# One tile in 128 of a graph kernel's gathered rows fetched by SyncE, a row at a time, and spilled blocks fetched two blocks ahead

## The chip, the cores and the metric

The kernel runs on one NeuronCore of a Trainium2 chip. Its time is the device time of one execution in microseconds (us), given as the median of three runs. A profile is one further execution, recorded by the hardware profiler, with a time of its own.

The engines are named as in the profile: PE (TensorE), DVE (VectorE), ACT (ScalarE), POOL (GpSimd) and SP (SyncE). SP computes nothing; it issues copies between DRAM and on-chip memory, each of which waits in SP's queue until its semaphores allow it. POOL issues the indirect copies (gathers), whose row addresses stand in a column of 128 numbers on chip.

## What is computed

A graph with 12500 nodes of 96 features and 412500 edges, sorted by destination. Each edge takes the source node's row, the destination node's row and four edge numbers through a linear layer with ReLU; the result is normalised over all edges and summed by destination:

```
node_feat = mlp(x, W_node, ...)                       # (12500, 96)
edge_feat = mlp(edge_attr, W_edge, ...)               # (412500, 96)
message   = concat([x[src], x[dst], edge_feat])       # (412500, 288)
message   = mlp(message, W_msg, ...)                  # (412500, 96)
agg       = segment_sum(message, dst, 12500)
x         = layernorm(x + agg + node_feat)
# mlp(h): h = relu(h @ W + b); gamma * (h - mean) * rsqrt(var + eps) + beta, over the rows
```

## The kernel before

**Tables.** The product of the message layer is split by its three inputs. `p_tab` holds x @ W_msg[source part] for all nodes, `q_tab` the same for the destination part, both in DRAM. An edge then needs one row of `p_tab` (384 bytes) by its source number. The source rows are scattered, so they are gathered; destination rows are neighbours, since the edges are sorted.

**Tiles, groups, blocks.** 128 edges are a tile, four tiles a group (`GT` = 4, 512 edges), four groups a block (`BG` = 4). There are 3223 tiles, 806 groups (`NG`) and 202 blocks. `gather(g, pg)` (L168) issues one gather of 128 rows on POOL for each tile of group g (L172).

**Stages.** While the tables and the statistics of nodes and edges are computed (up to about 630 us), POOL gathers the first 26 blocks and SP writes them back to DRAM (`spill`, 768 KB a block, L183). `SPILL` = 104 is the number of groups so treated. Then POOL fills a ring of `RING` = 21 group buffers (`ring`, tile `pg`, L341 and L364), and the message stage begins.

**The message stage** goes over all 202 blocks in the order `order`: the 176 blocks that are gathered late, with the 26 spilled ones strewn among them, one after about every seven. The order of the instructions on all engines is the one written in the loop (L523 to L547). For each step k, that is group g of the block at place s:

- at the first group of a block, `load(s + 2)` on SP: edge numbers (L408, L410, one set for two late blocks), then a register load of the block's first node (L413) and with it a copy of rows of `q_tab` into one of three slots of `rhs` (L418), which waits until PE has used the slot. Then `fetch(s + 1)`: if that block is a spilled one, its 768 KB come back from DRAM into one of two buffers `pb` (L425).
- `linear(k + 1)` on PE (L464), one group ahead, and `message(k)`: DVE adds the gathered rows (L475, tile `hs`), ACT applies the ReLU once a block (L482). `edges(s + 1)` (L450) and `prepare(s + 1)` (L457) make the next block's inputs of `linear`.
- `sums(k - 4)` on PE (L497) sums by destination, and `add` on DVE (L510, L511) adds a block's sums to the whole, two blocks later.
- if g is a late group, the gathers of group `ahead` = g + 21 (nearly; the last lines of the loop) into the ring slot that group g has just left.

Every copy that SP issues takes one of eight semaphores in turn and waits for the copy that had it before; POOL's gathers have eight others.

After the loop follow the statistics of the messages and the output in 13 pieces (L720 to L755). `general()` is a second way for other inputs, which these inputs don't take.

Of the kernel before, what the change touches and what calls it, by code (L numbers as in the profile page):

```python
# [11 lines left out]
F32 = mybir.dt.float32  # L12
I32 = mybir.dt.int32
# [3 lines left out]
ET = mybir.EngineType  # L17
# [3 lines left out]
N, C, E, ED = 12500, 96, 412500, 4  # L21
EPS = 1e-5
P = 128
# [3 lines left out]
GT, GE, BG = 4, 512, 4  # L27
NT = -(-E // P)
NG = -(-NT // GT)
NBL = -(-NG // BG)  # L30
NTP, NGP = NBL * BG * GT, NBL * BG
EP = NGP * GE
# [19 lines left out]
SPILL = 26 * BG  # L52
RING = 21
# [2 lines left out]
HB, RB = 2, 3  # L56
CL, CE = 2, 2
BUSY = 4
J = 8


# [12 lines left out]
def gnn(ctx, tc, t):  # L74
    nc = tc.nc
    const = ctx.enter_context(tc.tile_pool(name="const", bufs=1))
    dram = ctx.enter_context(tc.tile_pool(name="dram", bufs=1, space=DRAM))
    p_tab = dram.tile([NN, C], F32, name="p_tab")
# [11 lines left out]
    ring = rpool.enter_context(tc.tile_pool(name="ring", bufs=RING))  # L90
# [16 lines left out]
    wide = const.tile([P, P], F32, name="wide")  # L107
# [57 lines left out]
                (nc.scalar if (c // CH + k) % 2 else nc.sync).dma_start(outs[k][:, c:c + CH, :], r[:, :, k, :])  # L165
            yield

    def gather(g, pg):  # L168
        tab, idx = (t["x"], src_raw) if g < RAW * BG else (p_tab, src)
        for i in range(min(GT, NT - g * GT)):  # L170
            k = g * GT + i
            nc.gpsimd.indirect_dma_start(  # L172
                out=pg[:, i, :], out_offset=None, in_=tab[:, :],
                in_offset=bass.IndirectOffsetOnAxis(ap=idx[:, k:k + 1], axis=0))
        return pg
# [110 lines left out]
    def edge_norm():  # L286

        with tc.tile_pool(name="es", bufs=2) as work, tc.tile_pool(name="es1", bufs=1) as one, \
                tc.tile_pool(name="es_ps", bufs=4, space=PSUM) as ps:
            stats = one.tile([P, NS, NBL, 6], F32, name="estats")  # L290
            for b in range(NBL):
                if b % J == 0:
                    yield
                    ea = work.tile([P, J, GE], F32, name="ea")
                    n = min(J, NBL - b)
                    for i in range(NS):
                        nc.sync.dma_start(ea[Q * i:Q * i + 2 * EK, :n, :],
                                          t["ea"][EK * i:EK * (i + 2), b:b + n, :])
                for i in range(NS):
                    k = NS * b + i  # L300
                    if k % 2 == 0:
                        pr = ps.tile([P, 2, GE], F32, name="pr")
                    nc.tensor.matmul(pr[:, k % 2, :], wide[Q * i:Q * i + 2 * EK, :],  # L303
                                     ea[Q * i:Q * i + 2 * EK, b % J, :], start=True, stop=True)
                    if k % 2:
# [32 lines left out]
            nc.vector.tensor_scalar(w_e, w_msg[:, 2, :], a_e, None, op0=OP.mult)  # L338

    def fast(ring):  # L340
        def ahead_of(g):  # L341
            return gather(g, ring.tile([P, GT, C], F32, name="pg"))

        with tc.manual_schedule(engines={ET.SP, ET.Pool}):
            nc.sync.dma_start(q_tab[:WM, :], zero[:WM])
# [18 lines left out]
            got = {g: ahead_of(g) for g in range(SPILL, SPILL + RING)}  # L364
# [3 lines left out]
        order = []  # L368
# [7 lines left out]
        with tc.tile_pool(name="fix", bufs=1) as fix, tc.tile_pool(name="msg", bufs=2) as work, \  # L376
# [22 lines left out]
            def load(s):  # L399

                b = order[s]
                first = SPILL // BG
                c, o = ((b - first) // CL * CL + first, CL) if b >= first else (b // CE * CE, CE)
                if c not in eas:
                    o = min(o, NBL - c)
                    eas[c] = work.tile([P, o, GE], F32, name="ea" if b >= first else "eae")
                    for i in range(BG):
                        nc.sync.dma_start(eas[c][Q * i:Q * i + EK, :, :], t["ea"][EK * i:EK * (i + 1), c:c + o, :])  # L408
                    for i in range(2):
                        nc.sync.dma_start(eas[c][EK + i:P:Q, :, :], rel_d[i][:, c * BG * GE:(c + o) * BG * GE]  # L410
                                          .rearrange("o (b g e) -> (o g) b e", g=BG, e=GE))
                ea = eas[c][:, b - c, :]
                _, val = nc.values_load_multi_w_load_instructions(  # L413
                    base[:, b:b + 1], engines=[ET.SP], min_val=0, max_val=N - 1,
                    skip_runtime_bounds_check_because="they are nodes' numbers")
                rows = q_tab[bass.ds(val[0], WN), :]
                rows = bass.AP(rows.tensor, rows.offset, [[C, WN], [WS * C, BG], [1, C]], None, rows.runtime_checks)
                nc.sync.dma_start(rhs[C:C + WN, s % RB, :, :], rows)  # L418
                block[s] = ea

            def fetch(s):
                b = order[s]
                if b * BG < SPILL:
                    back = work.tile([P, BG, GT, C], F32, name="pb")
                    nc.sync.dma_start(back, spill[b].rearrange("p g (a c) -> p g a c", a=GT))  # L425
                    for i in range(BG):
                        got[b * BG + i] = back[:, i, :, :]
# [18 lines left out]
            def edges(s):  # L446

                prs[s] = ps.tile([P, BG, GE], F32, name="pr", bufs=1)
                for i in range(min(BG, NG - order[s] * BG)):
                    nc.tensor.matmul(prs[s][:C + WN, i, :], we[Q * i:Q * i + EK + 2, :],  # L450
                                     block[s][Q * i:Q * i + EK + 2, :], start=True, stop=True)

            def prepare(s):

                n = min(BG, NG - order[s] * BG)
                pr, x = prs[s], left[s % 2]
                nc.scalar.activation(x[:C + WN, :n, :], pr[:C + WN, :n, :], AF.Relu)  # L457

            def linear(k):
                s, g = steps[k]  # L460
                n = min(GT, NT - g * GT)
                zs[k] = zb[k % 2][:, :GT * C].rearrange("p (t c) -> p t c", c=C)
                for i in range(n):
                    nc.tensor.matmul(zs[k][:, i, :], left[s % 2][:KR, g % BG, i * P:(i + 1) * P],  # L464
                                     rhs[:KR, s % RB, g % BG, :], start=True, stop=True)

            def message(k):
                s, g = steps[k]
                n = min(GT, NT - g * GT)
                i = g % BG  # L470
                h, z, pg = hb[s % HB], zs.pop(k), got.pop(g)
                if i == 0:
                    four[0] = work.tile([P, BG, GT, C], F32, name="hs")
                hs = four[0]
                nc.vector.tensor_add(hs[:, i, :n, :], z[:, :n, :], pg[:, :n, :])  # L475
                if i == min(2, NG - 1 - (g - i)):
                    b = g - i
                    nc.vector.tensor_tensor(  # L478
                        h[:, :, :, C + 1:C + 1 + WN], rel[:, b:b + BG, :].unsqueeze(3).to_broadcast([P, BG, GT, WN]),
                        nodes_of.unsqueeze(2).to_broadcast([P, BG, GT, WN]), op=OP.is_equal)  # L480
                if i == BG - 1 and n == GT:
                    nc.scalar.activation(h[:, :, :, :C], hs, AF.Relu)  # L482
                elif i == BG - 1 or g == NG - 1:
                    for o in range(i + 1):
                        m = GT if o < i else n
                        nc.scalar.activation(h[:, o, :m, :C], hs[:, o, :m, :], AF.Relu)
# [13 lines left out]
            def add(s):  # L500
# [9 lines left out]
                    nc.vector.tensor_tensor(to, pa[:, i:n:2, C + 1:C + 1 + WN], to, op=OP.add)  # L510
                nc.vector.tensor_add(gram[:, :n, :], pa[:, :n, :C + 1], gram[:, :n, :])  # L511

            n, ahead = len(steps), SPILL + RING
            with tc.manual_schedule(engines={ET.SP, ET.Pool, ET.PE, ET.DVE, ET.Activation}):
                load(0)
                fetch(0)
                load(1)
                edges(0)  # L520
                prepare(0)
                linear(0)
                for k in range(n + SKEW):  # L523
                    s, g = steps[min(k, n - 1)]
                    if k < n and g % BG == 0:
                        if s + 2 < len(order):
                            load(s + 2)
                        if s + 1 < len(order):
                            fetch(s + 1)
                    if k + 1 < n:  # L530
                        linear(k + 1)
                    if k < n:
                        message(k)
                    if 0 <= k - BG < n:
                        sums(k - BG)
                    if k < n and s + 1 < len(order):
                        if g % BG == 0:
                            edges(s + 1)
                        if g % BG == 2:
                            prepare(s + 1)  # L540
                        if g % BG == 3 and order[s + 1] < RAW:
                            convert(s + 1)
                    if k >= SKEW and (k - SKEW) % BG == 0:
                        add((k - SKEW) // BG)
                    if k < n and g >= SPILL and ahead < NG:
                        got[ahead] = ahead_of(ahead)
                        ahead += 1  # L547

            d = fix.tile([C, BG, C], F32, name="d")
            s = fix.tile([C, 3], F32, name="s")  # L550
# [167 lines left out]
    with tc.tile_pool(name="fin", bufs=2) as work, tc.tile_pool(name="fin_ps", bufs=2, space=PSUM) as ps:  # L718

        busy = ps.tile([P, GE], F32, name="busy", bufs=1)  # L720
        for i in range(BUSY):
            nc.tensor.matmul(busy, ident, rel[:, i * P:(i + 1) * P, :].rearrange("p g t -> p (g t)"), start=True, stop=True)  # L722
# [67 lines left out]
```

## Time and profile before

| what | us |
|---|---|
| median of three runs | 4114.34 |
| lowest and highest | 4112.78, 4116.98 |
| the profiled execution | 4124.01 |
| its span, first to last instruction | 4122.3 |
| busy in the span: POOL, PE, DVE, ACT | 3072.2, 2875.0, 1245.9, 1035.6 |
| gathers of `pg`, 2807 | 2654.7 busy, 0.946 each |
| start of the first and the last gather of `pg` | 555.7, 4066.0 |
| first and last add of gathered rows (L475) | 633.5, 4068.8 |
| mean granted clock of PE | 0.728 of full speed |

The span is the time from the first to the last recorded instruction; the execution's own time lies 1.7 us above it. The share of busy time is a mean over stages: which wait ends last in a stage is read from the groups, whose lines give the busy time, the mean of one, the idle time just before them, and what ended most of it. An L with a number is a line of the kernel; a q behind an engine means its queue, where copies are issued. DMA share is the mean busy share of the 16 DMA engines.

### The profile page before, as it was taken

To read this page: it belongs to the slowest core of one execution; us is meant where nothing else is said; L and a number is where in the kernel's file an instruction comes from. 1 tells how busy PE (TensorE), PEld (TensorE's weight loads), DVE (VectorE), ACT (ScalarE), POOL (GpSimd) and SP (SyncE) were. 2 spreads that over 40 slices of the span, in tenths; PEclk is the share of its full clock that TensorE was granted. 3 is DMA by queue.
4 is the path that set the end of the run, shared out by engine and by line. 5 is a ranking of instruction groups with operands and counts; after the bars stand their busy time and mean duration, and the time that the engine had idled before them with its cause. 6 is when DMAs were issued, how large, how long until landed. Compare 5 with 4: busy or idle time off the path is not lost. (4 is left out here: it accounts for less than half of the span.)

```text
span 4122.3 us, 46288 instructions
## 1 busy us (share of the span) xinstructions
PE 2875.0 (70%) x16517; PEld 2372.3 (58%) x16517; DVE 1245.9 (30%) x2410; ACT 1035.6 (25%) x804; POOL 3072.2 (75%) x3244
## 2 busy tenths in 40 slices
PE   4699968776667766666576667766777667666666
PEld 4455537666556655655565556666666556555555
DVE  2599983222122222222122212221222122221223
ACT  1387753221112211111122111121211122211112
POOL 6777777777777777777777777777777777777775
PEclk7655558877677778778777777776777677878777
DMA  8555532222222222222222222222222222222224
GB/s 241 170 115 110 106 78 67 48 54 54 53 53 47 54 52 47 53 55 54 52 47 54 52 54 46 54 55 52 46 54 54 53 46 54 54 52 47 54 53 114
DMA packets 190373, 274.29 MB, mean 67 GB/s; under 512 B 121571, under 2 KB 121956, under 8 KB 189126
## 3 DMA queue, kind: packets, MB, share of 16 engines
q0 software_dynamic: 103136, 158.62, 18.4%
q1 hardware_dynamic: 71684, 99.14, 8.8%
q10 hardware_dynamic: 15312, 13.47, 1.2%
q8 instruction: 133, 2.18, 0.2%
q14 instruction: 108, 0.88, 0.1%
HBM read 227.55 MB, written 43.43 MB: 66 GB/s over the span
## 5 line engine op out<-in xcount | busy, mean ns | idle before, releaser
L172 POOL DMA_INDIRECT pg<-p_tab,src x2807 | 2654.7, 946 | 856.9 <-issue 766.0
L464 PE MATMUL z<-rhs,left 128*128 128x96 f32 x6446 | 1172.6, 341 | 1050.8 <-issue 613.3
L464 PEld LDWEIGHTS z<-rhs,left 128*128 128x128 f32 x6446 | 1063.0, 250 | 1312.7 <-issue 718.6
L475 DVE TENSOR_TENSOR hs<-z,pg 128x384 f32<-128x384 f32 x702 | 391.4, 557 | 2510.5 <-DMA pg<-p_tab,src 2199.7
L497 PE MATMUL pa<-h 128*97 128x128 f32 x6446 | 1112.4, 330 | 12.5 <-ACT h L482 9.0
L497 PEld LDWEIGHTS pa<-h 128*97 128x97 f32 x6446 | 989.7, 212 | 18.5 <-ACT h L482 15.2
L482 ACT ACTIVATE h<-hs 128x1536 f32<-128x1536 f32 x201 | 298.1, 1483 | 2018.3 <-DVE hs L475 2018.3
L457 ACT ACTIVATE left<-pr 127x2048 f32<-127x2048 f32 x202 | 378.4, 1873 | 716.8 <-PE pr L450 716.8
L172 POOL DMA_INDIRECT stage<-p_tab,src x368 | 352.8, 959 | 127.9 <-issue 107.7
L303 PE MATMUL pr<-ea,wide 10*128 10x512 f32 x1212 | 372.0, 1062 | 18.8 <-DMA ea<-in_ea 18.8
L309 DVE BATCH_NORM_STATS2 estats<-r 128x6 f32<-128x512 f32 x606 | 361.3, 676 | 25.5 <-ACT r L307 25.5
L307 ACT ACTIVATE r<-pr 128x1024 f32<-128x1024 f32 x303 | 293.1, 1024 | 141.8 <-PE pr L303 117.9
L303 PEld LDWEIGHTS pr<-ea,wide 10*128 10x128 f32 x1212 | 198.2, 319 | 191.3 <-ACT r L307 85.3
L450 PE MATMUL pr<-ea,we 7*127 7x512 f32 x1404 | 229.6, 725 | 12.8 <-DMA ea<-rel_d 12.8
L478 DVE TENSOR_TENSOR h<-rel,z 128x496 f32<-128x496 f32 x202 | 133.4, 660 | 0.0
L511 DVE TENSOR_TENSOR gram<-pa,gram 97x388 f32<-97x388 f32 x202 | 111.3, 551 | 0.0
L510 DVE TENSOR_TENSOR agg<-pa,agg 97x62 f32 x404 | 90.0, 223 | 36.8 <-PE pa L497 20.8
L475 DVE TENSOR_TENSOR hs<-z,pb 128x384 f32<-128x384 f32 x104 | 57.7, 555 | 114.7 <-PE z L464 114.7
L450 PEld LDWEIGHTS pr<-ea,we 7*127 7x127 f32 x1404 | 61.4, 205 | 43.2 <-issue 23.4
L172 POOL DMA_INDIRECT stage<-in_x,src_raw x48 | 45.6, 949 | 27.3 <-issue 10.7
L275 PE MATMUL py<-center,xp 96*128 96x96 f32 x196 | 42.8, 423 | 31.5 <-ACT xp L270 18.5
L275 PEld LDWEIGHTS py<-center,xp 96*128 96x128 f32 x196 | 42.0, 332 | 32.3 <-ACT xp L270 18.9
(113 smaller groups left out, 501.4 us busy)
## 6 DMA issues: line engine op xcount, KB each, us to landing
pg<-p_tab,src POOLq DMA_INDIRECT x2807
spill<-stage SPq DMA_DIRECT2D x26, 768.0 KB
pb<-spill SPq DMA_DIRECT2D x26, 768.0 KB
ea<-in_ea SPq DMA_DIRECT2D x75, 160.0 KB
rhs<-q_tab SPq DMA_DIRECT2D x202, 46.5 KB
ea<-in_ea SPq DMA_DIRECT2D x352, 20.0 KB
stage<-p_tab,src POOLq DMA_INDIRECT x368
y_d<-y0s SPq DMA_DIRECT2D x12, 384.0 KB
```

The lines of the kernel that those rows point to most:

```text
L172: nc.gpsimd.indirect_dma_start(out=pg[:, i, :], out_offset=None, in_=tab[:, :], in_offset=bass.IndirectOffsetOnAxis(ap=idx[:, k:k + 1], ax ...
L303: nc.tensor.matmul(pr[:, k % 2, :], wide[Q * i:Q * i + 2 * EK, :], ea[Q * i:Q * i + 2 * EK, b % J, :], start=True, stop=True)
L307: nc.scalar.activation(r, pr, AF.Relu)
L309: nc.vector.bn_stats(stats[:, (k - o) % NS, (k - o) // NS, :], r[:, 1 - o, :])
L450: nc.tensor.matmul(prs[s][:C + WN, i, :], we[Q * i:Q * i + EK + 2, :], block[s][Q * i:Q * i + EK + 2, :], start=True, stop=True)
L457: nc.scalar.activation(x[:C + WN, :n, :], pr[:C + WN, :n, :], AF.Relu)
L464: nc.tensor.matmul(zs[k][:, i, :], left[s % 2][:KR, g % BG, i * P:(i + 1) * P], rhs[:KR, s % RB, g % BG, :], start=True, stop=True)
L475: nc.vector.tensor_add(hs[:, i, :n, :], z[:, :n, :], pg[:, :n, :])
L478: nc.vector.tensor_tensor(h[:, :, :, C + 1:C + 1 + WN], rel[:, b:b + BG, :].unsqueeze(3).to_broadcast([P, BG, GT, WN]), nodes_of.unsqueeze ...
L482: nc.scalar.activation(h[:, :, :, :C], hs, AF.Relu)
L497: nc.tensor.matmul(pas[s][:, g % BG, :C + 1 + WN], h[:r, i, :C + 1], h[:r, i, :C + 1 + WN], start=i == 0, stop=i == n - 1)
L511: nc.vector.tensor_add(gram[:, :n, :], pa[:, :n, :C + 1], gram[:, :n, :])
```

## The change

The fourth tile of one group in 32 (`SG`), beginning with group 125, is not gathered by POOL. SP fetches its 128 rows with 128 copies of one row. Their numbers come as one row of the new input `rows` (the source numbers, a tile to a row) into `lin`, 128 numbers in the first row of the tile `wide`, which is not used otherwise any more at that point. A register load on SP takes 16 numbers (`SR`) into registers, and 16 copies use them as addresses. This is done at every second group (`SS`), so eight times in 16 of the 32 groups, at the end of the step, on SP's queue. After the last 16 the next tile's numbers are asked for. A period that would reach beyond the last group is left to POOL altogether.

Besides, `fetch` is called for the block two places on in the order, where it was one.

```diff
--- before.py
+++ after.py
@@ -56,6 +56,8 @@
 HB, RB = 2, 3
 CL, CE = 2, 2
 BUSY = 4
+SR, SS = 16, 2
+SG = 8 * BG
 J = 8
 
 
@@ -165,9 +167,9 @@
                 (nc.scalar if (c // CH + k) % 2 else nc.sync).dma_start(outs[k][:, c:c + CH, :], r[:, :, k, :])
             yield
 
-    def gather(g, pg):
+    def gather(g, pg, without=0):
         tab, idx = (t["x"], src_raw) if g < RAW * BG else (p_tab, src)
-        for i in range(min(GT, NT - g * GT)):
+        for i in range(min(GT, NT - g * GT) - without):
             k = g * GT + i
             nc.gpsimd.indirect_dma_start(
                 out=pg[:, i, :], out_offset=None, in_=tab[:, :],
@@ -338,8 +340,8 @@
             nc.vector.tensor_scalar(w_e, w_msg[:, 2, :], a_e, None, op0=OP.mult)
 
     def fast(ring):
-        def ahead_of(g):
-            return gather(g, ring.tile([P, GT, C], F32, name="pg"))
+        def ahead_of(g, without=0):
+            return gather(g, ring.tile([P, GT, C], F32, name="pg"), without)
 
         with tc.manual_schedule(engines={ET.SP, ET.Pool}):
             nc.sync.dma_start(q_tab[:WM, :], zero[:WM])
@@ -510,13 +512,28 @@
                     nc.vector.tensor_tensor(to, pa[:, i:n:2, C + 1:C + 1 + WN], to, op=OP.add)
                 nc.vector.tensor_add(gram[:, :n, :], pa[:, :n, :C + 1], gram[:, :n, :])
 
+            lin = wide[0:1, :].bitcast(I32)
+
+            def row_numbers(g):
+
+                nc.sync.dma_start(lin, t["rows"][g * GT + GT - 1:g * GT + GT, :])
+
+            def rows_of(pg, lo, hi):
+                _, val = nc.values_load_multi_w_load_instructions(
+                    lin[:, lo:hi], engines=[ET.SP], min_val=0, max_val=N - 1,
+                    skip_runtime_bounds_check_because="they are nodes' numbers")
+                for p in range(lo, hi):
+                    nc.sync.dma_start(pg[p:p + 1, GT - 1, :], p_tab[bass.ds(val[p - lo], 1), :])
+
 
 
             n, ahead = len(steps), SPILL + RING
+            row_numbers(ahead)
             with tc.manual_schedule(engines={ET.SP, ET.Pool, ET.PE, ET.DVE, ET.Activation}):
                 load(0)
                 fetch(0)
                 load(1)
+                fetch(1)
                 edges(0)
                 prepare(0)
                 linear(0)
@@ -525,8 +542,7 @@
                     if k < n and g % BG == 0:
                         if s + 2 < len(order):
                             load(s + 2)
-                        if s + 1 < len(order):
-                            fetch(s + 1)
+                            fetch(s + 2)
                     if k + 1 < n:
                         linear(k + 1)
                     if k < n:
@@ -543,7 +559,15 @@
                     if k >= SKEW and (k - SKEW) % BG == 0:
                         add((k - SKEW) // BG)
                     if k < n and g >= SPILL and ahead < NG:
-                        got[ahead] = ahead_of(ahead)
+                        m = (ahead - SPILL - RING) % SG
+                        if m == 0:
+                            by_row = ahead if ahead + SG <= NG else None
+                        got[ahead] = ahead_of(ahead, int(ahead == by_row))
+                        if by_row is not None and m % SS == 0 and m // SS * SR < P:
+                            lo = m // SS * SR
+                            rows_of(got[by_row], lo, min(lo + SR, P))
+                            if m // SS * SR == P - SR and by_row + 2 * SG <= NG:
+                                row_numbers(by_row + SG)
                         ahead += 1
 
             d = fix.tile([C, BG, C], F32, name="d")
@@ -764,6 +788,7 @@
     s, d = np.asarray(inputs["src"]), np.asarray(inputs["dst"])
     d = np.pad(d, (0, EP - E), mode="edge")
     give("src", np.pad(s, (0, EP - E)).reshape(NTP, P).T)
+    give("rows", np.pad(s, (0, EP - E)).reshape(NTP, P))
     give("dst", d.reshape(NTP, P).T)
     base = d[::GE * BG]
     give("base", base.reshape(1, NBL))
```

With the new lines L168, L172, L408 to L425, L464 and L475 of the kernel before are L170, L174, L410 to L427, L466 and L477 of the changed one; the table of numbers is loaded at L519, the registers at L522, the rows at L526.

## The prediction

> **What bounds the kernel now.** I read the busy line of the page first, then the costliest groups, then POOL's own waits, then the gathers stage by stage, and last SP's queue, which takes over the work. The first two (columns of a group: busy us, mean ns of one, idle before, its releaser):
>
> ```profile
> PE 2875.0 (70%) x16517; PEld 2372.3 (58%) x16517; DVE 1245.9 (30%) x2410; ACT 1035.6 (25%) x804; POOL 3072.2 (75%) x3244
> L172 POOL DMA_INDIRECT pg<-p_tab,src x2807 | 2654.7, 946 | 856.9 <-issue 766.0
> L475 DVE TENSOR_TENSOR hs<-z,pg 128x384 f32<-128x384 f32 x702 | 391.4, 557 | 2510.5 <-DMA pg<-p_tab,src 2199.7
> ```
>
> POOL is not busy all the time, 75%, and PE nearly as much. But DVE's add, which starts every group, sat 2199.7 us waiting for gathered rows, and the gathers waited for nothing: 2654.7 + 856.9 = 3511.6 us for 2807 of them is 1.251 us from one to the next, and the idle 0.305 us of each is "issue". POOL's waits and its timeline say the same (waits: us in total, times, longest; timeline: start, duration):
>
> ```profile
> POOL pg L172 <- issue: 766.0, 2512, 0.3
> POOL pg L172 <- DMA pg<-p_tab,src: 82.1, 266, 1.3
> POOL pg L172 <- DVE hs L475: 5.2, 17, 0.3
> ...
> 2002.32 0.94 POOL L172 DMA_INDIRECT pg<-p_tab,src  x1 [0.30 <-issue]
> 2003.57 0.95 POOL L172 DMA_INDIRECT pg<-p_tab,src  x1 [0.30 <-issue]
> 2003.77 0.56 DVE L475 TENSOR_TENSOR hs<-z,pg 128x384 f32<-128x384 f32 x1 [4.59 <-DMA pg<-p_tab,src]
> 2004.82 0.95 POOL L172 DMA_INDIRECT pg<-p_tab,src  x1 [0.30 <-DMA pg<-p_tab,src]
> ```
>
> The waits put down to a DMA or to DVE are the same 0.30 us: 82.1/266 and 5.2/17 are 0.31 us each, so nothing holds POOL. By stage (us, busy us of the gathers and their count, clock, DMA share, GB/s):
>
> ```profile
> 200.00:300.00 100.00, 74.01 (x80) 0.50 0.60 116
> ...
> 600.00:1000.00 400.00, 302.43 (x321) 0.76 0.24 56
> 1000.00:1500.00 500.00, 378.02 (x401) 0.76 0.23 51
> 3500.00:4000.00 500.00, 378.03 (x401) 0.79 0.23 52
> ```
>
> The pace is the same from the first to the last stage, 1.25 us, also where DMA is 60% busy. So the end is one chain: gathers of p_tab from 76 to 4067 us with hardly a gap (3175 x 1.251 = 3972 of 3991 us), then some 55 us of last group and output. A gather less on POOL is 1.251 us less, whatever else happens, unless POOL is made to wait.
>
> **SP, which takes the rows.** Its issues (min/median/max ns) and its largest wait:
>
> ```profile
> L418 SPq FUSED_REGOPS  x202: 37/37/51, 626.0 to 3997.0; - x101
> L418 SPq MOVE rhs<-q_tab x202: 29/29/39, 626.1 to 3997.1; - x101
> L418 SPq DMA_DIRECT2D rhs<-q_tab x202: 258/290/313, 626.2 to 4011.5; - x101
> L418 SPq EVENT_SEMAPHORE  x199: 17/17/17, 638.5 to 3997.1; - x199
> L413 SPq TENSOR_LOAD <-base x202: 432/656/894, 625.1 to 3996.4; - x101
> L198 SPq DMA_DIRECT2D b_msg<-in_L_gnn_b_msg x1: 259/259/259, 16.9 to 16.9; - x1
> L384 SPq DMA_DIRECT2D rhs<-bias x12: 571/590/597, 615.1 to 622.0; - x12
> SPq L418 <- PE z L464: 2800.2, 199, 31.6
> ```
>
> In the 3386 us from 626 to 4012 SP waits 2800.2 us for PE to free a rhs slot, so it works 586 us, 2.9 us a block.
>
> **The change part by part.**
> *Removed:* the fourth gather of groups 125, 157, ..., 765. The loop asks for a whole period of 32 groups (765 + 32 = 797, under 806), so 21; the changed kernel's instruction list has 2786 gathers of pg where there were 2807. 21 x 1.251 = 26.3 us off POOL.
> *Added on SP:* 21 loads of 128 row numbers, 168 register loads of 16 numbers each, 2688 copies of one row of 384 B, each with one register operation. One row: 259 ns for the copy (L198, the same shape, one row from DRAM), 37 + 29 for its address, 17 for its wait: 0.34 us. From above, 0.59 + 0.08 = 0.67 us (L384, the dearest small copy). I take 0.34, since L198 has the same direction and shape, and L418 shows that an address from a register costs no more (0.29).
> A register load of one number takes 0.656 us; for 16 at once the ends are 0.66 and 16 x 0.656 = 10.5 us. The Trainium skill, "DMA: Bandwidth & Descriptors", Latency and other measured facts, calls 600 ns the floor of such a load; a floor speaks for the low end, and I take 0.66.
> *The sum on SP:* a period of 32 gathered groups is 8 late blocks and 8 x 26/176 = 1.2 early ones, and POOL needs 127 x 1.251 = 158.9 us for it. SP needs 128 x 0.34 + 8 x 0.66 + 9.2 x 2.9 = 43.5 + 5.3 + 26.7 = 75.5 us. Within the active half, a block has 32 rows: 10.9 + 1.3 + 2.9 = 15.1 us, while POOL's four groups take 20 us. At 0.67 us a row it is 25.6 us, SP falls 22 us behind over four blocks and regains it in the idle half; the register loads at 10.5 us would make it 34.8 and 59 us. All of that is covered by the ring: POOL may run 21 groups, 105 us, ahead of DVE, and today DVE follows it at its heels (4.59 us idle before the add above).
> *Waits added:* the first row of a tile waits for DVE's add of the ring slot's last group; behind it on SP stand the next block's edge rows and its q_tab rows, for which PE waits (L450, L464). That add is at SP's own place in the order, and by then DVE has little before it, so up to one group, 5 us, once in 159. By the instruction list that row waits for gathers into earlier occupants of the slot, not for its own tile's three. On DVE, the add of such a group waits for eight more semaphores; the last rows are asked for seven groups, 35 us, before it. On POOL, the first gather into the slot 21 groups later waits for eight more: 21 x 8 x 17 ns = 2.9 us if seen, nothing if they fit in the 0.30 us of issue, as the one wait in four does today. I take nothing, and 2.9 for the range.
> *In the DMA engines:* a packet of the gathers takes 18.4% x 16 x 4122 / 103136 = 0.118 us, so 2688 rows are 0.5% of the engines' span against 23% busy. POOL's pitch at 0.60 share (200 to 300 us, 1.25 us) shows no price.
> A rule against the change: the same page, Anatomy of one DMA, gives every DMA on the gather's path about 2.0 us whatever its size, and "Perfetto Trace Analysis", DMA Optimizations, wants copies under 2 KB batched. One row after the other at 2.0 us is 256 us a tile: more than 158.9, and the kernel would be bound by SP, far slower. The trace has a landing: the last gather ends on POOL at 4066.95 and the add that needs it starts at 4068.79, 1.84 us later, as the rule says. But the wait list shows each row waiting only for the copy eight before it, so it comes to 2.0/8 = 0.25 us a row, under the 0.34 of issue. The first two q_tab copies show that one queue digests small rows in quick order:
>
> ```profile
> 626.15 1.32 SPq L418 DMA_DIRECT2D rhs<-q_tab  x2
> 627.53 4.11 SPq L408 DMA_DIRECT2D eae<-in_ea  x4
> ```
>
> They are 2 x 124 rows of 384 B; the issue behind them was held 3 us, after which it ran on: 248 rows within 5.5 us, 0.02 us a row.
> *Moved:* the fetch of a spilled block goes from one block ahead to two. It is a 768 KB copy, 0.8 us on SP, before q_tab rows no longer needed soon; its slot was last used by the early block two before, some 14 blocks ago, so it waits for nothing. Today's adds of spilled blocks (x104) wait for PE, not for the fetch; I cost it at 0. If it were late, the ring would cover 100 us.
> *What is late next:* POOL again, with 26.3 us less.
>
> **The rivals.**
> 1. Gain as counted, 4114.3 - 26.3 = 4088. For: POOL waits for nothing. Chance 0.72; own range 4084 to 4093.
> 2. Part is given back on POOL: semaphore waits (2.9 us), a pitch that rises by a few ns under the extra packets (5 ns x 2786 = 14 us), a lag of DVE that touches the ring at the start, where DVE begins at 633.5, 15.5 groups behind. 4093 to 4106. Against: the even pace at any DMA share. Chance 0.11.
> 3. No change: a pitch longer by 9 ns, or rows that reach POOL's chain in another way. Chance 0.04.
> 4. Slower: SP becomes the bound. The place is the row copy at SP's queue; it decides from (158.9 - 5.3 - 26.7)/128 = 0.99 us a row. At 1.2 us a period takes 186 us, 27 more; over 21 periods 567, less 100 for the ring, 4114 + 440 = 4560. At 2.0 us, 6600. For: nothing in the trace copies a DRAM row by a register address 16 times in a row, and copies at the start that stood behind large ones took 1 to 3 us. Against: 0.34 to 0.67 for every small copy that did not. With 10.5 us register loads it would decide from 0.38 us a row, near my own price. Chance 0.13.
> That the change does nothing is excluded by the 21 gathers missing from POOL's list.
>
> **How the numbers follow.** The profiled execution took 4124.0 us, span 4122.3; the median of three is 4114.3, 0.2% less, so 26.3 us of the profile is 26.2 there: 4088. Rival 1 and most of 2 hold 8 in 10: 4083 to 4100. Faster by over 0.2% (8.2 us, about what a measurement of this kernel can tell from no change) is 1 and 2: 0.83; within it 0.04; slower 0.13.
>
> **What would show it.** Right: 2786 gathers, mean 946 ns, pitch still 1.251 us, POOL waits all "issue" of 0.3 us, last gather start near 4040; SP row copies of 260 to 300 ns each, 16 in 5 to 6 us, DVE still waiting for pg. Wrong: DVE or PE waiting for the row copies or for ea and rhs, POOL waiting for DVE's add (a full ring), a pitch over 1.255 us, a row period near 1 us on SP, or a register load of several us.

## The result and the profile after

The changed kernel takes 4087.39 us (median of four runs, 4085.70 to 4088.15, the profiled one among them) where the kernel before takes 4114.26 (four runs, 4112.78 to 4116.98; its profiled execution, 4124.01, is not among them). The ratio is 0.9935, its 95% interval 0.9924 to 0.9947: 26.9 us less. The forecast was 4088.0.

The same parts of the profile of the changed kernel. First the page, the busy line and the groups (busy us, mean ns of one, idle before, its releaser):

```profile
PE 2965.9 (73%) x16517; PEld 2428.2 (59%) x16517; DVE 1244.8 (30%) x2410; ACT 1036.7 (25%) x804; POOL 3046.3 (75%) x3223
L174 POOL DMA_INDIRECT pg<-p_tab,src x2786 | 2628.8, 944 | 849.8 <-issue 764.3
L477 DVE TENSOR_TENSOR hs<-z,pg 128x384 f32<-128x384 f32 x702 | 391.5, 558 | 2465.0 <-DMA pg<-p_tab,src 2083.8
```

There are 21 gathers fewer, each as long as before, and the adds of DVE still wait for gathers. The waits of POOL (us in total, times, longest):

```profile
POOL pg L174 <- issue: 764.3, 2507, 0.3
POOL pg L174 <- DMA pg<-p_tab,src: 74.2, 242, 0.7
POOL pg L174 <- DVE hs L477: 5.8, 19, 0.3
```

Nothing has joined the chain: what is put down to a DMA or to DVE is again some 0.31 us each (74.2/242, 5.8/19; the longest 0.7, where it was 1.3), the ordinary time between two gathers. The stages show the same pace at a high and at a low DMA share (us, busy us of the gathers and their count, clock, DMA share, GB/s):

```profile
200.00:300.00 100.00, 74.99 (x81) 0.50 0.59 116
...
600.00:1000.00 400.00, 302.11 (x322) 0.75 0.24 56
1000.00:1500.00 500.00, 378.06 (x401) 0.75 0.23 53
3500.00:4000.00 500.00, 377.75 (x402) 0.72 0.23 51
```

What changed much is SP's queue. The lines of its new work (min/median/max ns, first and last start):

```profile
L526 SPq FUSED_REGOPS  x2688: 37/37/42, 633.1 to 3804.1; - x192
L526 SPq MOVE pg<-p_tab x2688: 29/29/38, 633.3 to 3804.2; - x192
L526 SPq DMA_DIRECT2D pg<-p_tab x2688: 224/225/288, 633.4 to 3804.3; - x192
...
L522 SPq TENSOR_LOAD <-wide x168: 1135/1222/1378, 631.8 to 3796.7; - x168
```

Its largest waits, where the slot of `rhs` stood at 2800.2 us before:

```profile
SPq L420 <- PE z L466: 1246.8, 111, 26.2
SPq L526 <- DMA pg<-p_tab,src: 156.5, 35, 11.2
```

And the timeline of SP through the first tile (start us, us from the first to the end of the last copy):

```profile
633.39 15.09 SPq L526 DMA_DIRECT2D pg<-p_tab  x32
...
653.83 14.66 SPq L526 DMA_DIRECT2D pg<-p_tab  x32
...
675.53 14.31 SPq L526 DMA_DIRECT2D pg<-p_tab  x32
...
692.82 14.24 SPq L526 DMA_DIRECT2D pg<-p_tab  x32
707.16 0.24 SPq L519 DMA_DIRECT2D wide<-in_rows  x1
```

SP gave up 1553 us of waiting (2800.2 to 1246.8), 74 us for each of the 21 tiles, and still waits 1246.8 us for PE. That is the spare time in which the rows were fetched.

**Where the time went, profile against profile.** The profiled executions took 4124.01 and 4087.16 us, 36.9 apart, more than the medians. The changed kernel's gathers, with the start of the first and the last:

```profile
L174 POOL DMA_INDIRECT pg<-p_tab,src x2786: 938/944/961, 552.6 to 4029.9; - x199
```

The first starts at 555.7 before and 552.6 after, the last at 4066.0 and 4029.9. So between them 3510.3 us became 3477.3, 33.0 less; the start gives 3.1, and the part behind the last gather, 56.3 against 55.5 us, gives 0.8. The pace of the gathers is (4066.0 - 555.7)/2806 = 1.2510 us before and (4029.9 - 552.6)/2785 = 1.2486 after: 21 gathers at 1.251 are 26.3 us, and 2785 gathers 0.0024 us faster are 6.7. The next section gives reasons to put this second part down to the execution and not to the change.

Three further sets, in which the kernel before itself took 5254 to 5300 us, stand at the end of the experiments, compared only among themselves; elsewhere it took its usual 4111 to 4124 us.

### The profile page after: what moved, and what is told of

Same layout as the page of the kernel before. It is cut to its first block, busy times and chain, and to the rows that moved or that the text cites. A ratio compares the mean times of both kernels' runs of the same rounds, so it can differ in the third digit from the quotient of the medians.

```text
span 4085.4 us, 54768 instructions
## 1 busy us (share of the span) xinstructions
PE 2965.9 (73%) x16517; PEld 2428.2 (59%) x16517; DVE 1244.8 (30%) x2410; ACT 1036.7 (25%) x804; POOL 3046.3 (75%) x3223
## 5 line engine op out<-in xcount | busy, mean ns | idle before, releaser
L174 POOL DMA_INDIRECT pg<-p_tab,src x2786 | 2628.8, 944 | 849.8 <-issue 764.3
L466 PE MATMUL z<-rhs,left 128*128 128x96 f32 x6446 | 1197.6, 346 | 889.0 <-DVE hs L477 451.4
L466 PEld LDWEIGHTS z<-rhs,left 128*128 128x128 f32 x6446 | 1077.2, 253 | 1183.4 <-DVE hs L477 615.6
L499 PE MATMUL pa<-h 128*97 128x128 f32 x6446 | 1155.5, 339 | 18.6 <-ACT h L484 15.9
L477 DVE TENSOR_TENSOR hs<-z,pg 128x384 f32<-128x384 f32 x702 | 391.5, 558 | 2465.0 <-DMA pg<-p_tab,src 2083.8
L499 PEld LDWEIGHTS pa<-h 128*97 128x97 f32 x6446 | 1026.7, 219 | 26.1 <-ACT h L484 23.3
L174 POOL DMA_INDIRECT stage<-p_tab,src x368 | 353.1, 959 | 127.3 <-issue 107.4
L452 PE MATMUL pr<-ea,we 7*127 7x512 f32 x1404 | 245.8, 773 | 45.2 <-DMA ea<-rel_d 45.2
L477 DVE TENSOR_TENSOR hs<-z,pb 128x384 f32<-128x384 f32 x104 | 57.7, 555 | 133.6 <-PE z L466 133.6
L174 POOL DMA_INDIRECT stage<-in_x,src_raw x48 | 45.4, 946 | 24.8 <-issue 11.0
```

What stands on the lines that cost most here:

```text
L174: nc.gpsimd.indirect_dma_start(out=pg[:, i, :], out_offset=None, in_=tab[:, :], in_offset=bass.IndirectOffsetOnAxis(ap=idx[:, k:k + 1], ax ...
L499: nc.tensor.matmul(pas[s][:, g % BG, :C + 1 + WN], h[:r, i, :C + 1], h[:r, i, :C + 1 + WN], start=i == 0, stop=i == n - 1)
```

## The experiments

**Fetch alone.** The kernel with the fetch two blocks ahead and all tiles gathered by POOL:

```diff
-                            by_row = ahead if ahead + SG <= NG else None
-                        got[ahead] = ahead_of(ahead, int(ahead == by_row))
+                            by_row = None
+                        got[ahead] = ahead_of(ahead)
```

> The spilled blocks are fetched two blocks ahead, and POOL gathers all tiles as before; no rows on SP. Theory (POOL's row of gathers sets the end, each worth 1.251 us): no change, 4114 us within 3, 2807 gathers. Rival (part of the gain comes from the earlier fetch): some us under 4110.

Measured: 4120.39 us, the kernel before on the same chip 4120.75; ratio 0.9997, interval 0.9988 to 1.0006. From its page:

```profile
L174 POOL DMA_INDIRECT pg<-p_tab,src x2807 | 2654.0, 945 | 856.8 <-issue 781.4
```

The fetch brings nothing and costs nothing that these runs can tell. The pace in its profile is 1.2507 us.

**Rows alone.** The row copies, with the fetch one block ahead as before:

```diff
-                fetch(1)
...
-                            fetch(s + 2)
+                        if s + 1 < len(order):
+                            fetch(s + 1)
```

> SP fetches the 21 tiles row by row, but the spilled blocks are fetched one block ahead as before. Theory: the whole gain, 4087.5 us within 3, since the ring covers a fetch that SP issues late by a block. Rival (the earlier fetch is needed once SP is busy): DVE and PE wait for pb, and if that reaches POOL it is 4092 us or more.

Measured: 4094.85 us against 4120.75 on that chip (the expected times count from 4114); ratio 0.9938, interval 0.9924 to 0.9951, 25.9 us less.

```profile
L174 POOL DMA_INDIRECT pg<-p_tab,src x2786 | 2628.7, 944 | 850.4 <-issue 772.0
...
L477 DVE TENSOR_TENSOR hs<-z,pb 128x384 f32<-128x384 f32 x104 | 57.6, 554 | 131.3 <-PE z L466 131.2
```

The rows are the whole gain, and the adds of spilled blocks (`pb`) wait for PE here too, not for their fetch: the earlier fetch isn't needed.

This run also bears on the pace. Its profiled execution took 4086.81 us at 1.2488 us a gather, its four other executions 4093.7 to 4095.5. So one program on one chip differs by 7 to 9 us from execution to execution, and the 0.0024 us between the two paces, 3202 times, would make 7.7. The profiles at the usual time lie at two places: 1.2510, 1.2507 and 1.2508 (before, fetch alone, and one in 64 below), and 1.2485 to 1.2488 (after, rows alone, rows left out, and one in 64 by 32). The difference is in the gather's own busy time, whose median is 947 ns in the first three and 944 in the others. One in 32 below has both medians in its two profiles, so the program alone doesn't decide it; what does, no run shows. The executions without a profile don't show their pace, so it is inferred that the two medians of the result, 4114.26 and 4087.39, have the same.

**The rows left out.** The 21 gathers are gone from POOL, and SP makes one plain copy of 128 rows in place of the 128 row copies. It is the first 128 rows of the table, so the computation of those tiles is changed:

```diff
-                            rows_of(got[by_row], lo, min(lo + SR, P))
+                            if m == 0:
+                                nc.sync.dma_start(got[by_row][:, GT - 1, :], p_tab[0:P, :])
```

> The 21 tiles get the first 128 rows of the table in one plain copy each instead of their own rows; the 2688 row copies and the register loads are left out. Theory: the row copies cost nothing, so the time is that of the change, 4087.5 us within 3. Rival (the row copies give back part of the gain, by contention in the DMA engines or waits): faster than the change by 3 us or more.

Measured: 4094.23 us against 4120.75; 0.9937, interval 0.9924 to 0.9951.

```profile
L174 POOL DMA_INDIRECT pg<-p_tab,src x2786 | 2628.8, 944 | 849.7 <-issue 775.1
```

With the rows it is 4094.85, without them 4094.23. The 2688 row copies and their register loads cost nothing that these runs can tell.

**One tile in 64.** Twice as many tiles by SP, 42 gathers off POOL; SP's active half becomes the whole time:

```diff
-SG = 8 * BG
+SG = 4 * BG
```

> One tile in 64 on SP: a tile every 16 groups, 16 rows at every second group all the time; 42 gathers less than before. POOL alone would give 4114.3 - 42 x 1.25 = 4062 us. SP's active blocks took 17.3 to 21.7 us in the trace of the change, and a block of early groups adds 0.6, so about 20.1 us a block against POOL's 19.7: theory, SP and POOL level, 4062 to 4075 us, DVE close to a full ring behind in places, POOL's waits for DVE appearing or not. Rival (SP's work stays hidden entirely): 4062 us within 3. Rival (SP is already the bound): over 4087 us.

Measured: 4076.64 us against 4120.75; 0.9894, interval 0.9878 to 0.9909, 44.1 us less. The waits:

```profile
POOL pg L174 <- DVE hs L477: 17.7, 58, 0.3
...
DVE hs L477 <- PE z L466: 1890.0, 557, 18.3
DVE hs L477 <- DMA pg<-p_tab,src: 324.1, 68, 15.0
PE pr L452 <- DMA ea<-rel_d: 657.4, 70, 15.0
SPq L420 <- PE z L466: 25.4, 7, 8.1
```

Read from the bottom: SP has no spare time left (25.4 us of waiting for PE, from 1246.8), PE waits for SP's copies, DVE waits for PE and no longer mainly for gathers. Yet POOL, the first line, waits for nobody: the ring takes up DVE's lag, and at the end DVE has caught up (the last gather starts at 4012.3, the last add of gathered rows at 4015.1). The gain falls short of 42 x 1.251 = 52.5 us all the same; the next run tells where.

**One tile in 64, numbers taken 32 at a time.** Half as many register loads, to free SP without touching POOL; the rows come in larger lots, at every fourth group, as well:

```diff
-SR, SS = 16, 2
-SG = 8 * BG
+SR, SS = 32, 4
+SG = 4 * BG
```

> One tile in 64 with 32 rows at every fourth group, once more. Theory (SP's queue was level with POOL with 16 at a time, which cost 8 us at the end): where the kernel before takes its usual 4114 to 4121 us, 52 us less than it, and DVE waiting for POOL's gathers. Rival (the 8 us are lost with the number of rows): 44 us less.

Measured: 4066.02 us (four runs, 4064.01 to 4070.18) against 4112.67; 0.9890, interval 0.9873 to 0.9906, 46.65 us less. It is the fastest kernel of the study, 21 us below the changed one.

```profile
L522 SPq TENSOR_LOAD <-wide x168: 2022/2086/2259, 629.9 to 3841.8; - x168
L174 POOL DMA_INDIRECT pg<-p_tab,src x2765: 940/944/961, 550.8 to 4002.0; - x198
```

```profile
DVE hs L477 <- DMA pg<-p_tab,src: 1528.4, 385, 13.7
DVE hs L477 <- PE z L466: 758.9, 267, 18.0
```

This did relieve SP, which waits 120.6 us for PE again (25.4 in the last kernel), and DVE waits mostly for gathers. But against the kernel before it gained no more than the 44.1 us of the last kernel, within the intervals. So a DVE that is late at the end, by which I had explained the missing 8 us, is not the cause. Two profiles at one pace, fetch alone and one in 64 by 16, say where the time is lost:

```profile
L174 POOL DMA_INDIRECT pg<-p_tab,src x2807: 940/947/962, 554.2 to 4063.7; - x188
L174 POOL DMA_INDIRECT pg<-p_tab,src x2765: 940/947/962, 555.2 to 4012.3; - x198
```

From the first to the last gather 3509.5 us became 3457.1, 52.4 less: the 42 gathers are gained whole. The first gather starts 1.0 us later, and the part behind the last one grows from 58.0 us (span 4121.7) to 62.8 (span 4075.1), 4.8 more; 46.6 is left, which is how far apart the two executions are (4123.44 and 4076.84). So the loss is in the end of the program. POOL's last instructions are drains, after its last output work. The kernel before, the changed kernel and this one, each from the answer on the program's last line (min/median/max ns, first and last start):

```profile
L786 POOLq DRAIN  x3: 40/113/4145, 4117.3 to 4122.0; - x3
L786 SPq DRAIN  x3: 7/7/13, 4120.6 to 4121.7; - x3
```

```profile
L811 POOLq DRAIN  x3: 40/113/2428, 4081.0 to 4085.2; - x3
L811 SPq DRAIN  x3: 7/7/13, 4084.6 to 4084.9; - x3
```

```profile
L811 POOLq DRAIN  x3: 40/113/9368, 4052.9 to 4062.8; - x3
L811 SPq DRAIN  x3: 7/7/13, 4056.4 to 4062.5; - x3
```

SP's first drain comes when its last output has landed; the end of the span follows 0.8 us behind that or behind POOL's long drain, whichever is later, in every profile of this study. Before, POOL's began at 4117.3 and was through at 4121.5, 0.9 us behind SP's at 4120.6, and the span ended at 4122.3. After, it was through at 4083.4, ahead of SP's 4084.6: it cost nothing. Here it was through at 4062.3, 5.9 us behind SP's (in the pair above, 0.7 us behind in fetch alone and 5.8 in one in 64). So 52.5 us should arrive as 52.5 - 5.0 = 47.5; 46.65 and 44.1 were measured, and both intervals hold 47.5. The intervals alone would not decide it, since that of this run reaches to 52 us, close to 52.5; the profiles do. From after to this one, both at 1.2486 us, the last gather starts 27.9 us earlier (4029.9 to 4002.0) and the part behind it is 5.6 longer (55.5 to 61.1), 22.3 in all, as their times are apart (4087.16 - 4064.83).

**The sets in which the kernel before took 5254 to 5300 us.** Three sets of runs fell here, on three chips. One of these chips gave the kernel before 4112.67 us in one set (beside one in 64 by 32) and 5300.0 in a later one (beside one in 32), so the chip alone doesn't make it. The changed kernel as it stands, twice:

> The changed kernel itself once more, beside the kernel before on the same chip. Both theories: ratio 0.9935 as the first time, that is 26 to 27 us less; as the mark for the others of this row.

> The changed kernel once more, as the mark for the next one, on a chip where the kernel before takes its usual time. Both theories: 26 to 27 us less than before.

All gathers on POOL, and the row copies made besides, into a tile that isn't read any more (nothing of the result depends on them):

```diff
-                    nc.sync.dma_start(pg[p:p + 1, GT - 1, :], p_tab[bass.ds(val[p - lo], 1), :])
+                    nc.sync.dma_start(iota.rearrange("p b w -> p (b w)")[p:p + 1, :C], p_tab[bass.ds(val[p - lo], 1), :])
...
-                        got[ahead] = ahead_of(ahead, int(ahead == by_row))
+                        got[ahead] = ahead_of(ahead)
```

> POOL gathers all 2807 tiles as before, and SP fetches the 2688 rows as in the change, but into a tile that nobody reads. Theory (the rows cost nothing on the path): the time of the kernel before within 3 us. Rival (the row copies slow POOL or the DMA engines by some ns a gather): 5 to 14 us more than before.

One in 64 with 32 numbers at a time, the edit of the run above, twice:

> As one tile in 64, but 32 rows at every fourth group and so one register load where there were two: from 0.656 us for one number and 1.222 for 16 a load of 32 comes to 1.8 us, 0.6 us less a block for SP. Theory (one in 64 lost 8 us to SP's queue, which was level with POOL, so that DVE was late at the end): SP falls under POOL's pace, DVE is at POOL's heels at the end, 52 us less than before, against 44 with 16 at a time. Rival (the 8 us are lost elsewhere, in the number of rows itself): 44 us less again.

> As one tile in 64, but 32 rows at every fourth group, so one register load where there were two: from 0.656 us for one number and 1.222 for 16, a load of 32 comes to 1.8 us, 0.6 us a block less for SP. Theory (one in 64 with 16 at a time lost 8 us because SP's queue was level with POOL and DVE was late at the end): 52 us less than before, DVE waiting for POOL's gathers again. Rival (the 8 us are lost with the number of rows): 44 us less again.

One in 32, twice:

```diff
-SR, SS = 16, 2
-SG = 8 * BG
+SR, SS = 16, 1
+SG = 2 * BG
```

> One tile in 32 on SP: a tile every 8 groups, 16 rows at every group; 84 gathers less. Theory (SP is bound): a block takes 64 x 0.416 + 4 x 1.22 + about 4.6 = 36 us on SP against 19.4 on POOL; 170 blocks x 36 = 6100 us from 633, with the end some 6700 to 6900 us, and POOL waiting for DVE's adds (a full ring). Rival (POOL stays the bound): 4114 - 84 x 1.25 = 4009 us.

> One tile in 32 on SP, 16 rows at every group, 84 gathers less than before. Theory (SP becomes the bound, and POOL waits on a full ring for DVE, DVE for PE, PE for copies of SP): 16 rows with their register load took 16 x 0.416 + 1.22 = 7.9 us in the change's trace, a block has four of these and 4.5 us of other work, 36 us against POOL's 19.4; 168 blocks x 36 from 633 us, then 70 us for the last groups and 55 to the end: 6800 us, between 6500 and 7100. Rival (POOL stays the bound): 4114 - 84 x 1.25 = 4009 us.

| kernel | us | kernel before | ratio, interval |
|---|---|---|---|
| the change | 5605.7 | 5294.3 | 1.059, 1.057 to 1.062 |
| the change | 5527.4 | 5254.6 | 1.052, 1.048 to 1.055 |
| rows besides | 5577.7 | 5294.3 | 1.052, 1.049 to 1.054 |
| one in 64 by 32 | 6251.8 | 5294.3 | 1.179, 1.176 to 1.183 |
| one in 64 by 32 | 6214.8 | 5254.6 | 1.183, 1.180 to 1.186 |
| one in 32 | 8800.3 | 5294.3 | 1.663, 1.657 to 1.668 |
| one in 32 | 8779.3 | 5300.0 | 1.656, 1.651 to 1.661 |

A gather still takes 0.943 us there, but SP's queue pauses between instructions: from one row copy to the next it is mostly 0.4 us, as at the usual time, or about 0.7, 1.4, 2.1 or 2.8. The timeline of SP in the changed kernel, and a wait of POOL with its longest instance:

```profile
1511.97 32.98 SPq L526 DMA_DIRECT2D pg<-p_tab  x32
...
1547.48 23.05 SPq L526 DMA_DIRECT2D pg<-p_tab  x32
...
1644.42 29.96 SPq L526 DMA_DIRECT2D pg<-p_tab  x32
...
1676.93 44.49 SPq L526 DMA_DIRECT2D pg<-p_tab  x32
```

```profile
POOL pg L174 <- DVE hs L477: 1047.1, 180, 101.6
...
970.30 0.94 POOL L174 DMA_INDIRECT pg<-p_tab,src  x1 [101.63 <-DVE hs L477]
```

In these lines 32 rows take 23 to 44 us in place of 14.6, up to 1.4 us a row, on either side of the 0.99 from which the fourth rival decides. And POOL now waits for DVE's add, that is on a full ring: once for 101.6 us, before the first add (969.5) and the first row copy (972.9), which is not the rows' doing, and later for up to 31 us at a time, all through the stage. How much of that the kernel before has here too isn't shown: it has no profile in these sets.

The run with the rows besides tells SP's new work from the missing gathers. It leaves all gathers on POOL and is about as much slower, by 283 us to the change's 311. So the work on SP's queue costs, and 21 gathers fewer give nothing back. With twice the rows (one in 64 by 32) the loss is 957 and 960 us, so it grows with the rows. The loss that the fourth rival names thus happens here. That SP alone sets the pace isn't shown: in the changed kernel's profile it still waits at least 470 us for PE. How dear SP as the bound is at the usual time, which the expectations asked of one in 32, these runs do not answer. That stays open, as does what makes the pauses.

## Why the prediction was right

**The 21 gathers.** Right: 1.251 us each, 26.3 us, against 25.9 (rows alone) and 26.5 (rows left out: 4120.75 - 4094.23). The rest of the change's 26.9 us may be the end of the program, which profile to profile gives 0.8; it is less than the medians can tell. The last gather was put near 4040 and started at 4029.9. The difference is the pace of the execution (7 us) and the earlier first gather (3 us), which the medians' difference of 26.9 has no room for. That the time itself, 4088, was met within 1 us is in part luck: in the next sets the kernel before took 4120.75 us and rows alone 4094.85, outside the 4084 to 4093 of the first rival, with a difference of 25.9. And three of the six sets of runs fell where the change loses; that the result came from one of the other three is luck too. The prediction had given 0.13 to slower.

**POOL's waits.** Taken at nothing, with 2.9 us kept for the range: nothing, the waits are 0.31 us on average and at most 0.7.

**The work on SP.** The cover was right and the sizes were not. The copy itself took 0.225 us, less than the 0.259 of L198. But a row took (14.66 - 1.22)/32 = 0.42 us, with one register load inside the 32 rows, for 0.34 predicted: the sum of the three instructions, 0.225 + 0.037 + 0.029 = 0.29, leaves out the gaps between them. A register load of 16 numbers took 1.222 us, not 0.66; for 32 it is 2.086. I had leaned on the low end because the Trainium skill ("DMA: Bandwidth & Descriptors", Latency and other measured facts) calls 600 ns the floor of such a load. The measurements differ: the 0.656 of L413 is the middle between two halves, 101 loads of 0.43 to 0.55 us and 101 of 0.77 to 0.89, those that follow the copies of L410, so half of the loads lie under the floor and none took 0.656. And the load grows by some 0.05 us a number: (2.086 - 1.222)/16 = 0.054, and (1.222 - 0.49)/15 = 0.049 if one number is taken at the middle of the shorter half. And the first rows of the tiles waited 156.5/21 = 7.5 us a tile, for "up to one group, 5 us". So an active block took 20.4, 21.7 and 17.3 us (the starts 633.39, 653.83, 675.53 and 692.82) for 15.1 predicted: SP keeps level with POOL's 20 us in that half, it has no lead. The tile cost SP 74 us of waiting for 48.8 in my sum. Two of these errors, 0.08 us a row and 0.56 us a load, are 10 + 4.5 us a tile; the waits at the first rows add 7.5; some 3 us are left. All of it stayed free for the reason given: the idle half, and the ring behind it. One in 64 shows how close that is: SP's spare time was gone.

**The rule of 2.0 us a DMA** ("DMA: Bandwidth & Descriptors", Anatomy of one DMA, as the prediction cites it). It was divided by the eight copies in flight, 0.25 us. The copies came 0.42 us apart, and SP's wait list has no row that waited for the copy eight before it, so it didn't show.

**The fetch.** Costed at 0 and measured at 0 (fetch alone), and not needed either (rows alone).

**What was not in the sum.** POOL's drain at the end. It cost 0.9 us before, nothing in the changed kernel and 5.9 in one in 64; the prediction treated the 55 us behind the last gather as fixed.

**The rivals.** No give-back on POOL: the pace fell from before to after (1.2510 to 1.2486) and is the same in fetch alone and one in 64 (1.2507, 1.2508). The fourth rival's point of 0.99 us a row is far from 0.42 at the usual time; in the three sets at its end some rows crossed it. Its 6600 us at 2.0 us a row should be 6700 by the same sum, which changes nothing.

## What to carry to other kernels

Where descriptors issued by one engine set the time, and its pace doesn't bend with the load of the DMA engines, count its issues: each one moved to a queue with idle time is worth its full pitch, even if the replacement is 128 small copies. Measure the spare time of the queue that takes them as its own waits, cost each copy from start to start and not by the sum of its instructions, and keep a reserve: a saving of 0.65% turned into a loss of 5 to 6% where that queue paused. When a sum comes out short by a few us, look at the last microseconds of the program before explaining it by the loop.

## What the runs showed of the hardware that was not expected

- POOL's long drain at the end goes with how many gathers the program made, the early ones included: 5.86 us with 3138 gathers, 9.37 with 3181, 2.43 with 3202, 4.15 with 3223. It is the same within 0.004 us in all profiles with one count, with row copies on SP or without. From 3202 to 3223 and from 3138 to 3181 it rises by 0.082 us a gather; in between it falls back. What it does isn't shown by any run.
- The pace of the gathers, over a whole execution, was near 1.2486 us in four profiles and near 1.251 in three; the gather's median, 944 or 947 ns, was both in two executions of one program (one in 32). Whether there are values between, no run shows.
- A register load from on-chip memory on SP took 1.222 us for 16 numbers and 2.086 for 32 (medians); for one number it took 0.43 to 0.55 us or, right behind the copies of L410, 0.77 to 0.89.
- In the sets at 5254 to 5300 us, SP's row copies came 0.4 us apart or later by about 0.7 us or a multiple of it.
